# Mixture-of-experts groups that pass their slots to and fro and keep weights, with additions placed after their gathers, in a four-layer attention and expert stack

## The chip, the cores and the metric

The kernel runs on one core of one Trainium2 chip, as one launch. The metric is the device time in microseconds of that core; the time of a kernel is the median of several runs. All arithmetic is float32.

## The reference, cut to what matters

The input is an image batch of 2 x 256 channels x 32 x 32, so 2 images (b = 0, 1) of 1024 tokens with 256 features. Two convolutional attention layers come first (layers 0 and 1), and nothing in them is changed. Then the tokens `t` go through two more layers:

```python
t = t + _L2_attn_ref(_ln_t(t), ...)   # window attention
t = t + _L2_ffn_ref(_ln_t(t), ...)    # 8 experts, top 2, hidden 1024, per-expert norm
t = t + _L3_attn_ref(_ln_t(t), ...)   # additive attention
t = t + _L3_ffn_ref(_ln_t(t), ...)    # 8 experts, top 2, hidden 512
# additive attention: for each pair of tokens i, j of one image
h = jnp.tanh(q[:, :, None, :] + k[:, None, :, :] + bh)   # 1024 x 1024 x 32
e = jnp.einsum('biju,u->bij', h, Wa[:, 0]) + ba[0]
v = softmax(e) @ inputs
# experts: h = gelu(x @ W1[e] + b1[e]); y = h @ W2[e] + b2[e]; sum of the two, weighted by the gate
```

## The kernel before

The changed part is the class `Late`, which computes everything behind the window attention. It is cut into steps that are Python generators; each `yield` ends a piece. The method `run` holds a table `plan` of the steps with a start, an end and a number of pieces, and `merge` issues the pieces of all steps in order of these planned times. The unit is about a microsecond, but only the order that results counts. The names of the steps are used throughout: the first digit is the layer, the second the group of tokens. In layer 2 there are two groups, one for each image (8 tiles of 128 tokens each). In layer 3 group 0 is image 0 (8 tiles), and groups 1 and 2 are the halves of image 1 (4 tiles each).

- **D** (`dispatch`): layer norm (`norm`, `inverse_root`), a transpose by TensorE (`ps_tr`), gate logits (`ps_router`), and `route`, some sixty small VectorE instructions with one counting product on TensorE (`ps_counts`) that give each token two slots. Then each tile's rows are scattered into `slots_in` in device memory, by two indirect DMAs a tile on GpSimd's queue. Last the experts' second bias is added to the tokens (`ps_wT`, `ps_b`).
- **E** (`experts`): loops over slot tiles of 128 rows ("slots" below), 23 in a group of 8 token tiles and 15 in a group of 4; 99 in all. A slot is loaded (`xr`), transposed (`ps_x`, then `xe` on VectorE), multiplied up (`ps_h`, bias `hb` on VectorE, Gelu `h` on ScalarE), multiplied down (`ps_y`, copied to `y` on VectorE) and stored to `slots_out`. The weights of a slot's expert come by indirect DMA into one of three lanes (`ew`): lane m % 3 walks its own third of the slots in ascending order of expert, and where the expert of a lane stays the same the index is put out of bounds and nothing is loaded. Each call of `experts` takes six new weight tiles, and its first three slots always load.
- **C** (`collect`): per token tile two indirect gathers from `slots_out` (`got`, L1425, GpSimd's queue) and two scaled additions into `t` (L1438, VectorE). In layer 2 it goes on to the norm, transposes and projections (`ps_p`, `kT`, `qb`) that the additive attention of that image needs; in layer 3 `finish` transposes four tiles of `t` at a time (`ps_f`), copies them (`y_f`, one buffer) and stores 128 channels of 512 tokens by one or two DMAs.
- **A** (`additive`): one step per image. `tanh(s)` issues four ScalarE activations of 128 x 1024 (a "set"), 64 sets an image; `products(s)` the eight TensorE matmuls that reduce them (`ps_e`). The tanh tiles have 8 buffers, so ScalarE can be two sets ahead of TensorE. After sets 32, 56 and 64 the softmax of 4, 3 and 1 token tiles is taken on ScalarE (`sc_a`); for each tile follow the transposes `ps_pt`, the values `ps_v` and an addition into `t`.

TensorE and ScalarE execute in the order that `merge` wrote from A0's start on. VectorE's, GpSimd's and the DMA queues' orders, and all orders ahead of A0, are left to the framework's scheduler, which orders by its own estimates. Every engine executes its queue in order, so a waiting instruction holds all that is behind it.

```python
"C20": (self.collect(2, 0), ("E20",), 172, 205, 20),
"E21": (self.experts(2, 1), ("D21",), 172, 450, 72),
"A1": (self.additive(1), ("C21", "A0"), 506, 815, 67),
"E30": (self.experts(3, 0), ("D30",), 550, 690, 50),
"E31": (self.experts(3, 1), ("D31", "E30"), 744, 830, 34),
"E32": (self.experts(3, 2), ("D32", "E31"), 846, 905, 34),
```

Of the kernel before, what the change touches and what calls it, by code (L numbers as in the profile page):

```python
# [44 lines left out]
}  # L45
SLOT_TILES = {IT: 2 * N // TILE + E - 1, IT // 2: N // TILE + E - 1}
NTILES = SLOT_TILES[IT]

# [7 lines left out]
def slot_tile(m, n):  # L56
    return m % LANES * -(-n // LANES) + m // LANES
# [946 lines left out]
class Late:  # L1004
# [3 lines left out]
    def __init__(self, ctx, stack, t):  # L1008
# [23 lines left out]
        for n in SLOT_TILES.values():  # L1032
            run = -(-n // LANES)
            self.tiles[n] = tl(f"tiles{n}", [P, run * LANES])
            iota(self.tiles[n], [[1, run], [run, LANES]], 0, 0)
# [52 lines left out]
    def norm(self, dst, src, tiles):  # L1088
# [6 lines left out]
        yield  # L1095
# [5 lines left out]
        yield  # L1101
# [11 lines left out]
    def normed(self, key, tokens, half):  # L1113

        if half == 0:
            self.u[key] = self.early.tile([P, IT, C], F32, name="u", bufs=3)[:, : len(tokens), :]
        tiles = range(4 * half, 4 * half + 4)
        yield from self.norm(
            lambda i: self.u[key][:, i, :], lambda i: self.t[:, tokens[i], :], tiles
        )  # L1120
        self.channels(key, tiles)
        yield
# [3 lines left out]
    def gate(self, l, b, half):  # L1126
# [14 lines left out]
        yield  # L1141

    def dispatch(self, *key, done=0):
# [11 lines left out]
        nc, t = self.nc, self.t  # L1155

        before = []
        for i in range(n):
# [9 lines left out]
            yield  # L1168

        for first in range(0, n, 4):  # L1170
# [15 lines left out]
    def route(self, key, count):  # L1186
# [14 lines left out]
        yield  # L1201
        yield
        nc.scalar.activation(lg, lg, AF.Exp)
        yield
# [4 lines left out]
        for hot in (h0, h1):  # L1209
# [8 lines left out]
            yield  # L1218
# [10 lines left out]
        yield  # L1229
# [12 lines left out]
        yield  # L1242
# [17 lines left out]
        yield  # L1260
        shape_t = [P, slot_tiles, E]
        whose, index = tl("rt_whose", shape_t), tl("rt_index", [P, slot_tiles])
        nc.vector.tensor_tensor(whose, over_tokens(ends, shape_t), broadcast(self.tiles[slot_tiles][:, :slot_tiles], shape_t), ALU.is_le)
# [7 lines left out]
        same, later = tl("rt_same", [P, slot_tiles - LANES]), slice(LANES, slot_tiles)  # L1271
        nc.vector.tensor_tensor(same, index[:, later], index[:, : slot_tiles - LANES], ALU.is_equal)
        nc.vector.tensor_scalar(index, index, float(P), self.part, ALU.mult, ALU.add)
        nc.vector.scalar_tensor_tensor(index[:, later], same, float(E * P), index[:, later], ALU.mult, ALU.add)
        rows = tl("rt_rows", [P, slot_tiles], U32, 2)
        nc.vector.tensor_copy(rows, index)
        yield
# [19 lines left out]
        yield  # L1297

    def experts(self, *key):
# [11 lines left out]
        raw, turned, hidden, waiting = {}, {}, {}, []  # L1311
        loaded = [
            [sb.tile([P, WIDEST[k]], F32, name=f"ew{k}", bufs=LANES) for k in range(2)] for _ in range(LANES)
        ]

        def fetch(m, k):
            if m >= slot_tiles:
                return
            w, width = loaded[m % LANES][k], packed[k].shape[1]
# [6 lines left out]
        def inputs(m):  # L1326
            if m >= slot_tiles:
                return
            raw[m] = sb.tile([P, C], F32, name="xr", bufs=3)
            at = slot_tile(m, slot_tiles) * TILE  # L1330
            nc.sync.dma_start(out=raw[m], in_=xs[at : at + TILE, :])
# [23 lines left out]
        def up(m, k):  # L1355
            w, x = loaded[m % LANES][0], turned[m]
# [16 lines left out]
        def down(m):  # L1373
            h = hidden.pop(m)
            w2 = loaded[m % LANES][1][:, : HB * C].rearrange("p (j d) -> p j d", j=HB)
# [7 lines left out]
            at = slot_tile(m, slot_tiles) * TILE  # L1383
# [7 lines left out]
        yield  # L1391
        turn(0)
        turn(1)
        yield
        for k in range(HB // 4):
            up(0, k)
            yield
# [15 lines left out]
    def collect(self, *key):  # L1413

        nc, t, (l, b) = self.nc, self.t, key
        tokens = GROUPS[key]
        n = len(tokens)
        shares, slots = self.routes[key][1:3]
        got = {}

        def gather(i):
            got[i] = []
            for slot in slots:
                y = self.sb.tile([P, C], F32, name="got", bufs=8)
# [4 lines left out]
                got[i].append(y)  # L1429

        for i in range(4):
            gather(i)
            yield
        for half in range(n // 4):
            for i in range(4 * half, 4 * half + 4):
                to = t[:, tokens[i], :]
                for y, share in zip(got.pop(i), shares):
                    nc.vector.scalar_tensor_tensor(to, y, share[:, i : i + 1], to, ALU.mult, ALU.add)  # L1438
                if i + 4 < n:
                    gather(i + 4)  # L1440
                yield
            if l == 2:
                yield from self.normed(("a", b), tokens, half)
                self.project(b, half)
            else:
                self.finish(tokens[4 * half])
            yield

    def finish(self, first):

        nc, t, b, at = self.nc, self.t, first // IT, first % IT * P
        for c in range(CC):
            ps = self.misc([P, CH], "ps_f")
            for k in range(CH // P):
                nc.tensor.transpose(  # L1455
                    ps[:, k * P : (k + 1) * P], t[:, first + k, c * P : (c + 1) * P], self.ident
                )
            y = self.sb.tile([P, CH], F32, name="y_f", bufs=1)
            nc.vector.tensor_copy(y, ps)  # L1459
            to = self.stack.out[b, c * P : (c + 1) * P, :]  # L1460
            n = min(CH, N - SHIFT - at)
            nc.sync.dma_start(out=to[:, at + SHIFT : at + SHIFT + n], in_=y[:, :n])  # L1462
            if n < CH:
                nc.sync.dma_start(out=to[:, : CH - n], in_=y[:, n:])
# [28 lines left out]
    def additive(self, b):  # L1493
# [69 lines left out]
        for s in range(IT * G + 1):  # L1563
# [10 lines left out]
            if jobs:  # L1574
                jobs.pop(0)()
        softmax(ready)
# [6 lines left out]
    def run(self, route):  # L1583
# [4 lines left out]
        self.p_x, self.p_h, self.p_y, self.p_e = psum("lt_x", 1), psum("lt_h", 2), psum("lt_y", 1), psum("lt_e", 1)  # L1588

        plan = {  # L1590
            "D20": (route, (), -12, 0, 14),
# [116 lines left out]
```

## Time and profile before

| | us |
|---|---|
| median of 6 runs (2997.58 to 3003.34) | 3000.36 |
| the profiled execution, its own time | 2997.72 |
| its span | 2996.0 |
| TensorE matmul busy in the span | 2743.4 (92%) |
| ScalarE busy | 1926.8 (64%) |
| VectorE busy | 1967.9 (66%) |

The profiled execution lies 1.7 us above its span and 2.6 us below the median. The stages behind the window attention, by their place in the span: E20 runs from 1912 to 2094, the first tanh starts at 2140.8, the last tanh ends at 2845.5, E32's first transpose is at 2910.0, its last product ends at 2973.3. In the trace each float32 product appears as two matmul records (32 records of `ps_h` and 16 of `ps_y` for a slot of layer 2, half of each in layer 3); transposes appear once. The columns of a table of stretches are: bounds in the span, length, then busy time and count of instructions of PE (TensorE), PEld (its weight loads), DVE (VectorE), ACT (ScalarE) and POOL (GpSimd), the mean granted clock of TensorE as a share of full speed, the DMA engines' share and GB/s.

### The profile page before, as it was taken

Reading aid. Unit: us, or ns where it says so; the run is one execution under the profiler, and the core shown is the slowest. Engines: PE = TensorE matmul, PEld = TensorE weight load, DVE = VectorE, ACT = ScalarE, POOL = GpSimd, SP = SyncE. Lnnn points to the kernel's source line nnn. Section 1 sums busy time; section 2 is a strip of 40 time slices with the busy share of each in tenths; the row PEclk is TensorE's granted clock in tenths of the full one; section 3 lists DMA queues with packets and bytes.
Section 4 is the critical chain, followed back from the end, with each engine's and each line's share of the span. In section 5 each row is a group of like instructions: output and inputs, shape, how many; then the busy total and the mean of one; then the engine's idle time right before and its main releaser. Section 6 shows DMA issues by size and latency. Waiting matters only on the chain. (4 is left out here: it accounts for less than half of the span.)

```text
span 2996.0 us, 78725 instructions
## 1 busy us (share of the span) xinstructions
PE 2743.4 (92%) x33062; PEld 1744.9 (58%) x33062; DVE 1967.9 (66%) x3673; ACT 1926.8 (64%) x2835; POOL 479.1 (16%) x569
## 2 busy tenths in 40 slices
PE   7899999999999999979999877799899989996967
PEld 4466656566656666645555445698566643663656
DVE  5898989898989898748778767643422334223343
ACT  1787888887878787735555522111499788987811
POOL 3000000000000000001111123442311122323233
PEclk9999999999999999989999988799899999998978
DMA  3000000000000000011101010344321112322335
GB/s 128 2 3 3 3 3 3 3 3 3 3 3 3 3 3 3 3 54 31 23 20 23 2 27 1 133 159 152 99 78 63 41 34 70 92 73 101 99 114 149
DMA packets 185043, 135.70 MB, mean 45 GB/s; under 512 B 134176, under 2 KB 162480, under 8 KB 180336
## 3 DMA queue, kind: packets, MB, share of 16 engines
q0 software_dynamic: 36864, 85.93, 8.8%
q1 hardware_dynamic: 146384, 44.27, 6.6%
q8 instruction: 260, 4.26, 0.5%
q10 hardware_dynamic: 1440, 0.47, 0.1%
q14 instruction: 95, 0.78, 0.1%
HBM read 181.24 MB, written 29.49 MB: 70 GB/s over the span
## 5 line engine op out<-in xcount | busy, mean ns | idle before, releaser
L177 ACT ACTIVATE sc<-sc,sa_shift 128x1024 f32<-128x1024 f32 x512 | 585.2, 1148 | 50.5 <-DMA sa_shift<-sa_min 50.3
L1506 ACT ACTIVATE th<-kT,qb 128x1024 f32<-128x1024 f32 x512 | 541.2, 1135 | 90.1 <-PE ps_e L1515 77.1
L140 PE MATMUL ps_s<-kT,qT 64*32 64x512 f32 x8192 | 503.9, 595 | 9.3 <-ACT sc L150 8.5
L216 PE MATMUL ps_o<-wt,v 128*64 128x128 f32 x6144 | 502.2, 276 | 0.0
L190 DVE STREAM_TRANSPOSE wt<-sc 128x768 f32<-128x768 f32 x512 | 465.7, 943 | 0.9 <-ACT sc L177 0.9
L216 PEld LDWEIGHTS ps_o<-wt,v 128*64 128x64 f32 x6144 | 441.1, 137 | 42.5 <-issue 42.5
L150 ACT COPY sc<-ps_s 128x1024 f32<-128x1024 f32 x256 | 257.5, 1006 | 117.5 <-PE ps_s L140 42.4
L1364 PEld LDWEIGHTS ps_h<-xe,ew 128*128 128x128 f32 x2320 | 278.8, 195 | 62.2 <-issue 37.1
L161 DVE TENSOR_REDUCE sa_least<-sc 128x1 f32<-128x1024 f32 x256 | 306.0, 1195 | 1.7 <-ACT sc L150 1.7
L147 DVE TENSOR_SCALAR_CACHE_REDUCE sc<-ps_s 128x1024 f32<-128x1024 f32 x256 | 301.3, 1177 | 5.9 <-PE ps_s L140 5.9
L1364 PE MATMUL ps_h<-xe,ew 128*128 128x128 f32 x2320 | 293.6, 281 | 10.1 <-DVE xe L1343 8.6
L1515 PE MATMUL ps_e<-th,pick 128*32 128x512 f32 x2048 | 278.9, 620 | 11.1 <-DVE ir_half L1079 9.8
L1378 PE MATMUL ps_y<-ew,h 128*128 128x256 f32 x1160 | 271.5, 383 | 4.6 <-ACT h L1353 2.6
L1369 DVE TENSOR_TENSOR hb<-ps_h,ew 128x512 f32<-128x512 f32 x145 | 100.2, 691 | 240.1 <-PE ps_h L1364 199.9
L216 PE MATMUL ps_o<-wl,v_odd 128*64 128x128 f32 x2048 | 250.9, 276 | 0.0
L1378 PEld LDWEIGHTS ps_y<-ew,h 128*128 128x128 f32 x1160 | 212.4, 190 | 60.9 <-issue 18.2
L1353 ACT ACTIVATE h<-hb 128x512 f32<-128x512 f32 x145 | 90.1, 623 | 240.7 <-DVE hb L1369 240.6
L140 PEld LDWEIGHTS ps_s<-kT,qT 64*32 64x32 f32 x8192 | 126.2, 106 | 201.5 <-issue 167.9
L198 PEld LDWEIGHTS ps_t<-ident,sc 128*128 128x128 f32 x1024 | 107.4, 140 | 215.6 <-issue 166.9
L644 ACT ACTIVATE sc<-sc,l_least 128x1024 f32<-128x1024 f32 x128 | 146.7, 1147 | 126.8 <-DVE sc L631 126.4
L216 PEld LDWEIGHTS ps_o<-wl,v_odd 128*64 128x64 f32 x2048 | 220.2, 137 | 0.0
L227 POOL TENSOR_TENSOR diag<-ident,sa_rec 32x128 f32<-32x128 f32 x64 | 24.9, 389 | 1170.4 <-DVE sa_rec L224 1170.4
(277 smaller groups left out, 3499.0 us busy)
## 6 DMA issues: line engine op xcount, KB each, us to landing
xr<-slots_in SPq DMA_DIRECT2D x99, 128.0 KB, 2.4
slots_out<-y SPq DMA_DIRECT2D x99, 128.0 KB, 1.7
sa_got<-sa_least SPq DMA_DIRECT2D x512, 0.5 KB, 1.8
sa_shift<-sa_min SPq DMA_DIRECT2D x512, 0.2 KB, 1.7
slots_in<-zero POOLq DMA_DIRECT2D x46, 128.0 KB, 2.2
sa_sums<-sa_total SPq DMA_DIRECT2D x256, 1.0 KB, 1.8
kh<-kh SPq DMA_DIRECT2D x32, 128.0 KB, 2.3
qh<-qh SPq DMA_DIRECT2D x32, 128.0 KB, 2.3
```

The source lines that it names most:

```text
L140: nc.tensor.matmul(ps[r][S * c : S * (c + 1), a, :].rearrange("p (b i) -> p b i", i=S), lhsT=qT[half, p, S * i : S * (i + 1)], rhs=keys[ha ...
L147: nc.vector.tensor_scalar(scores[m][0], flat[0], 1.0, None, ALU.mult, ALU.min, accum_out=least[m // 2][:, 0, h : h + 1])
L150: nc.scalar.copy(scores[m][1], flat[1])
L161: nc.vector.tensor_reduce(least[m // 2][:, 1, h : h + 1], scores[m][1], AX.X, ALU.min)
L177: nc.scalar.activation(scores[m][r], scores[m][r], AF.Exp, bias=shift[m // 2][:, r : r + 1], scale=-1.0, accum_out=total[i][:, 2 * p + r, ...
L190: nc.vector.transpose(weights[i, h][:, 2 * p + r, :], scores[m][r][:, :DIRECT])
L216: nc.tensor.matmul(sums[i][64 * k : 64 * (k + 1)], lhsT=values, rhs=w, start=(h == 0 and j == 0 and t == 0), stop=(h == 1 and j == 1 and t ...
L644: nc.scalar.activation(scores[n][r], scores[n][r], AF.Exp, bias=least[n][:, r : r + 1], scale=-1.0, accum_out=total[n // 4][:, at : at + 1],)
L1364: nc.tensor.matmul(ps[:, j, :], lhsT=a[:, c, at : at + P], rhs=x[:, c, :], start=(c == 0), stop=(c == CC - 1),)
L1378: nc.tensor.matmul(ps, lhsT=h[:, j, :], rhs=w2[:, j, :], start=(j == 0), stop=(j == HB - 1))
L1506: nc.scalar.activation(h, keys, AF.Tanh, bias=self.qb[b][:, s // G, g : g + 1])
L1515: nc.tensor.matmul(pe[i][c * U : (c + 1) * U, a, :], lhsT=self.pick[:, k, :], rhs=h[:, a, :], start=(k == 0), stop=(k == G - 1),)
```

## The change

- **To and fro.** Groups (2, 1) and (3, 1) (`BACK`) walk their slots in descending order, with the lanes mirrored. The six weight tiles are made once in `run` and kept over all groups. `route` remembers the last expert of each lane (`latest`), and a group in `FOLLOWS` compares its first slot of each lane with it, so that these loads too are skipped where the expert is the same. This costs a memset or a comparison and three one-column copies on VectorE for each group, and two more index tables at the start.
- **Additions once gathered.** `collect` issues its gathers first, in C20 all 16 and in C32 all 8 into tanh buffers, and its additions a set number of units later, 2.5 apart; statistics, scaling, transposes and projections have places of their own. VectorE's order too is now the written one, and from E21's start instead of A0's.
- **The plan.** Each step has a start and a distance between pieces, and a `yield` may give its own. E21 runs at 2.43 up to 205 and then at 4.8 (before: 3.86). A1 needs only "A0 tanh". D30's scatter pieces are 0.5 apart, and the bias additions become steps of their own (`shift`: B30, B31, B32). E30 starts at 582 with 4.4 between its two pieces a slot (before: 550 and 2.8). E31 also needs "A1 tanh": none of it is issued before A1's last set.
- **Output tile by tile.** `finish` handles one token tile: two transposes, one copy of 128 x 256 into a buffer of `got`, one DMA (two at an image's end), of 128 columns a row instead of 512.

```diff
-def slot_tile(m, n):
-    return m % LANES * -(-n // LANES) + m // LANES
+def slot_tile(m, n, back):
+    at = m % LANES * -(-n // LANES) + m // LANES
+    return n - 1 - at if back else at
+
+def lane(m, back):
+    return LANES - 1 - m % LANES if back else m % LANES
...
+        if key in FOLLOWS:
+            nc.vector.tensor_tensor(same[:, :LANES], index[:, :LANES], latest, ALU.is_equal)
+        else:
+            nc.vector.memset(same[:, :LANES], 0.0)
+        at = {lane(m, key not in BACK): m for m in range(slot_tiles - LANES, slot_tiles)}
+        for m in range(LANES):
+            nc.vector.tensor_copy(latest[:, m : m + 1], index[:, at[m] : at[m] + 1])
...
         def fetch(m, k):
-            w, width = loaded[m % LANES][k], packed[k].shape[1]
+            w, width = self.loaded[lane(m, back)][k], packed[k].shape[1]
...
+        if l == 3:
+            for i in range(4):
+                gather(i)
+            yield 9.0 if wide else 16.0
+            for i in range(n):
+                add(i)
+                if i + 4 < n:
+                    gather(i + 4)
+                yield 2.5
+                if i == 3 and n > 4:
+                    yield 9.0
+            return
+        if wide:
+            for i in range(n):
+                gather(i)
+            yield 8.5
+            for i in range(n):
+                add(i)
+                yield 2.5
+                if i == 3:
+                    scale(0)
+                if i == 5:
+                    channels(0)
+                if i == 6:
+                    self.project(b, 0)
...
+    def finish(self, i):
+        nc, b, at = self.nc, i // IT, i % IT * P
+        ps, y = self.misc([P, CC, P], "ps_f"), self.sb.tile([P, C], F32, name="got", bufs=8)
         for c in range(CC):
...
+            nc.tensor.transpose(ps[:, c, :], self.t[:, i, c * P : (c + 1) * P], self.ident)
+        y = y.rearrange("p (c n) -> p c n", c=CC)
+        nc.vector.tensor_copy(y, ps)
+        to = self.stack.out[b].rearrange("(c p) n -> p c n", p=P)
+        n = min(P, N - SHIFT - at)
+        nc.sync.dma_start(out=to[:, :, at + SHIFT : at + SHIFT + n], in_=y[:, :, :n])
+        if n < P:
+            nc.sync.dma_start(out=to[:, :, : P - n], in_=y[:, :, n:])
...
+        self.issued.add(f"A{b} tanh")
+        yield 9.0
         softmax(ready)
...
+            "E21": (self.experts(2, 1), ("D21", "E20"), 172, lambda now: 2.43 if now < 205 else 4.8),
+            "C20": (self.collect(2, 0), ("E20",), 172, 2.0),
+            "A0": (self.additive(0), ("C20",), 211, 4.75),
+            "N30": (self.gate(3, 0, 0), ("A0 half",), 420, 6.0),
+            "C21": (self.collect(2, 1), ("E21",), 471, 2.0),
+            "A1": (self.additive(1), ("C21", "A0 tanh"), 515, 4.6),
+            "D30": (self.dispatch(3, 0, done=1), ("A0", "N30"), 515, 2.0),
+            "E30": (self.experts(3, 0), ("D30",), 582, 4.4),
+            "B30": (self.shift(3, 0), ("D30",), 650, 6.0),
+            "D31": (self.dispatch(3, 1), ("A1 half", "D30"), 725, 2.0),
+            "C30": (self.collect(3, 0), ("E30", "B30"), 790, 2.0),
+            "E31": (self.experts(3, 1), ("D31", "E30", "A1 tanh"), 825, 1.9),
+            "B31": (self.shift(3, 1), ("D31",), 780, 3.0),
+            "D32": (self.dispatch(3, 2), ("A1", "D31", "C30"), 830, 2.0),
+            "E32": (self.experts(3, 2), ("D32", "E31"), 880, 1.9),
...
-        merge(plan["A0"][2])
+        merge(plan["E21"][2])
         engines = mybir.EngineType
-        with self.tc.manual_schedule(engines={engines.PE, engines.Activation}):
+        with self.tc.manual_schedule(engines={engines.PE, engines.Activation, engines.DVE}):
```

## The prediction, made before the change was run

> **What bounds the kernel now.** First the busy time of each stage behind the window attention (stretches of the span; the columns are in the section on the profile).
>
> ```profile
> 1912.00:2094.00 182.00, 181.22 (x1227) 168.58 (x1228) 84.47 (x245) 33.00 (x50) 62.86 (x63) 0.98 0.46 157
> 2094.00:2140.80 46.80, 33.15 (x166) 25.38 (x165) 28.36 (x89) 3.18 (x6) 21.31 (x22) 0.82 0.38 125
> 2140.80:2845.50 704.70, 658.73 (x4397) 395.23 (x4395) 224.40 (x607) 606.66 (x628) 158.97 (x162) 0.96 0.23 73
> 2845.50:2910.00 64.50, 40.40 (x246) 32.20 (x244) 29.24 (x114) 8.94 (x12) 25.34 (x26) 0.80 0.26 79
> 2910.00:2973.30 63.30, 59.85 (x398) 55.13 (x398) 22.58 (x46) 10.62 (x16) 26.13 (x27) 0.96 0.66 206
> 2973.30:2996.00 22.70, 2.78 (x9) 1.47 (x8) 5.68 (x11) 0.00 (x0) 7.67 (x8) 0.56 0.25 75
> ```
>
> E20 is pure TensorE (181 of 182 us). The tanh stage has two near limits: TensorE busy 659, ScalarE 607 of 705 us. Around it lie stretches where neither works. Second, what TensorE and VectorE waited for from 1912 and 2094 on, and what ScalarE waited for in the tanh stage (total, times, longest).
>
> ```profile
> PE ps_x L1339 <- DMA xr<-slots_in: 25.7, 4, 19.5
> PE ps_tr L1110 <- DVE u L1098: 18.0, 4, 11.0
> PE ps_f L1455 <- DVE t L1438: 13.8, 4, 7.6
> PE ps_e L1515 <- DVE ir_half L1079: 9.8, 1, 9.8
> PE ps_h L1364 <- DVE xe L1343: 8.6, 1, 8.6
> PE ps_b L1181 <- DVE wT L1175: 7.5, 2, 6.7
> ...
> DVE t L1438 <- DMA got<-slots_out,rt_slot: 45.2, 43, 5.4
> ...
> ACT th L1506 <- PE ps_e L1515: 77.1, 34, 9.1
> ```
>
> VectorE stood 45.2 us at additions whose gathers had not landed; `xe`, `u` and `wT` behind them kept TensorE (18.0 + 9.8 + 8.6 + 7.5), and ScalarE ran out of tanh tiles (77.1). No row has TensorE waiting for weights. Third, the timeline at the end.
>
> ```profile
> 2971.36 1.97 PE L1378 MATMUL ps_y<-ew,h 128*128 128x256 f32 x8 [0.56 <-issue]
> 2976.33 0.97 POOL L1425 DMA_INDIRECT got<-slots_out,rt_slot  x1 [11.51 <-issue]
> 2987.97 0.48 DVE L1438 SCALAR_TENSOR_TENSOR t<-got,rt_share,t 128x256 f32<-128x256 f32 x1 [0.79 <-DMA got<-slots_out,rt_slot]
> 2989.02 0.69 DVE L1459 COPY y_f<-ps_f 128x512 f32<-128x512 f32 x1 [0.57 <-PE ps_f L1455]
> 2992.08 0.69 DVE L1459 COPY y_f<-ps_f 128x512 f32<-128x512 f32 x1 [2.37 <-DMA out<-y_f]
> ```
>
> Behind the last product come a store, eight gathers at 1.27 us, additions, and two copies through one buffer.
>
> **Prices on TensorE.** From the timeline at full clock: a slot of layer 3 is 1.78 (`ps_h`, 16 records) + 0.22 + 1.73 (`ps_y`, 8) = 3.73 us, one of layer 2 twice the products, 7.3; a group of `ps_e` 1.92; one token tile's `ps_pt` and `ps_v` 1.09 + 3.62 = 4.7. On ScalarE: a set of tanh 4.23 (541.2 us / 128), a Gelu 0.55 in a row of tanh, a table load 1.28. The counts below are those of the two programs' instruction orders.
>
> **Up to 2094: +1 us.** Layers 0 and 1 and E20's order stay. A group's `route` gains a memset or comparison and three copies, at 0.17 us (the `rt_ends` copies) 0.7 us; only D20's lie ahead of E20's first load, the others beside TensorE work.
>
> **E20's end to the first tanh: 46.8 to 48 us.** Before, 16 of E21's products `ps_y` ran here and TensorE stood 13.3 us (8.58 + 0.73 + 3.96). Now 40 do. Until the first `ps_e` group TensorE has 192 records of `ps_h` (21.4), 80 of `ps_y` (17.3), 12 `ps_x` (1.3), 16 transposes (2.3) and the projections (7.7): 50; the first tanh is 5 earlier, as half a slot stands in between; and I allow 3 because additions every 2.5 units keep step with gather pairs (2 x 1.27), so that a late first one stays late. The stage is no shorter, but takes 22 us of TensorE work out of the next.
>
> **The tanh stage: 704.7 to 652 us.** ScalarE was busy 606.7 and idle 98.0. Between the first and last tanh there are now 15 Gelus fewer (58 against 73: three slots of E21 went ahead, nine Gelus of E31 behind) and one table load fewer: 8.3 + 1.3, so 597. TensorE gives up 62 us of slots here and falls to under 600. What idle time stays:
> - the softmax stretches, where TensorE has 4 x 4.7 us extra in eight sets. Eight sets of A0 with their slots cost TensorE 50.3 and ScalarE 44.2, the next eight 38.4 against 36.0, A1's 47.5 against 43.1: 6.1 + 2.4 + 4.4 = 13;
> - A0 to A1: the norm's second half, transposes, projections and `qb` follow A0's last group: 2 (that group) + 1.3 (the maximum, ahead in VectorE's order) + 1.4 (`uT`) + 3.9 (`ps_p`) + 1.4 (`qb`) = 10;
> - E30's start, which the new plan makes worse. Before, `ps_counts` at 2509.96 was followed by E30's first transpose at 2540.74, 30.8 us for slot numbers, 16 scatters and a load, covered by seven `ps_e` groups and the bias additions. Now four groups, 17 to 18 us of tanh, stand between, the biases are gone to B30, and VectorE's maximum of A1's tile 0 stands inside `route` and waits for one of these groups (+5). TensorE stands some 17 us at `ps_x` with the groups behind it; ScalarE is two sets (8.5) ahead and loses 17 + 5 - 8.5 = 14;
> - coupling. A0's first 32 sets took 161.1 us, and summing the dearer engine over each eight sets gives 149; the new mix is less dense, so I take 6 there and 7 for the rest: 13;
> - small waits, 5.
>
> Together 55, so 652. The cover for everything moved here is tanh; where it fails, the price is one to one.
>
> **Last tanh to last product: 127.8 to 143 us.** 30 slots now (before 19): 111.9; the last `ps_e` group 1.9; tile 7's `ps_pt` and `ps_v` 4.7; D32's transposes, router and count 3.4; biases 2.6; output transposes 3.7; 128 in all. E32 took 63.3 for 15 x 3.73 = 56, so 9 go on top for 30 slots. The 24 us hole ahead of E32 (3.83 + 0.77 + 19.54) shrinks because D32 runs inside E31: from its `ps_counts` TensorE still has five down and three up products, 14.6 us, plus 2 for a late `hb`; VectorE needs 7 to the slot numbers, GpSimd eight scatters and one weight load in its queue (11.5), then landing and load 4.5: 23. So 6 remain. On GpSimd's queue C31's gathers wait for E31's stores with E32's fetches behind them; three fetches are ahead, and a fetch lands in 3.2 us of a 3.73 slot.
>
> **Tail: 22.7 to 19.3 us.** The gathers keep their pace. After the last addition come two transposes, a copy (0.42) and two DMAs for one tile; the second `y_f` copy and its wait (2.37 + 0.69 + 0.3) go: 3.4. Rows of 512 bytes, and in the last tile of 384 and 128, take the place of 2 KB rows: the 128-byte rows landed in 1.9 us, the 1920-byte rows in 2.1, so nothing is added; between ends of 0 and +2 (twice the rows in one DMA) I take 0. The Trainium skill ("DMA: Bandwidth & Descriptors", Specifications) asks for at least 512 B a transfer, and would have the last tile's rows pay a read-modify-write; by it the tail would lose a microsecond or two of its gain, and the measured landings do not show it.
>
> **Kept weights: 0.** Up to nine slots' loads fall away, but no TensorE wait on weights is there to remove.
>
> **The clock.** TensorE's granted clock is 0.80 to 0.82 in the rows with holes, 0.96 and more elsewhere; the 16 records at 2113.74 took 4.00 us instead of 1.78 after an 8.58 us hole. Filled holes return that too, and my prices at full clock contain it.
>
> **The sum.** 2094 + 1 + 48 + 652 + 143 + 19.3 = 2957, 39 below the span of 2996.0. The profiled execution's own time would be 2959, and with the 2.6 us to the median 2961.
>
> **Rivals.**
> 1. More is filled than I allow: E30's start is covered after all and the coupling disappears (-27), and E32 finds its input (-6): 2928. For it: A1's stretch 2549.7 to 2658.7 had ScalarE busy 101.5 of 109 with a denser mix. Against it: the four groups are in the order.
> 2. Slower: ScalarE's idle time does not fall. VectorE's order is now fixed, and a copy, maximum or addition that stands ahead of its operand holds every `hb` and `xe` behind it, as the 45.2 us did; E30's start then costs 50 us rather than 14, say. Since 41 us of slots went behind the tanh, the break-even is an idle time of 55 + 39 = 94 us, nearly the old 98; at 110 the time is 3016. For it: the maximum inside D30's `route`. Against it: the additions of C20 to C32 stand 8.5 to 16 units behind their gathers, and eight gathers take 10.2 us.
> 3. It does not do what it says: the lanes' experts differ at the group borders and all loads stay. Then E31 and E32 start with 3.2 us for a load on an empty lane: 2964 to 2967, no change of sign. I count it within the forecast.
>
> **How the numbers follow.** Forecast (tanh stage within 15 us of 652, tail as said: 2942 to 2985) 0.69, rival 1 0.15, rival 2 0.16, of which half ends within 0.2% or better. 0.2% (6 us) is about what a measurement of this kernel can tell from no change. So faster 0.87, same 0.04, slower 0.09. The range takes in most of rival 1 and rival 2 up to an idle time of 86: 2930 to 2992.
>
> **What would show it.** Right: ScalarE's idle time in the tanh stage between 40 and 75 us, the longest wait of TensorE in it at E30's first `ps_x`; VectorE's wait on gathers under 15 us; a wait for `xr` at E32 of 3 to 10 us; one copy behind the last addition. Wrong: ScalarE still waiting 77 us for `ps_e`, or a tanh stage over 690 us.

## The result, and the profile after

The changed kernel took 3009.42 us (median of 21 runs) against 3000.26 us for the kernel before (42 runs): a ratio of 1.0027, 95% interval 1.0022 to 1.0033. It is slower by 0.27%, where 2961 us and a gain of 1.3% were forecast. The profiled execution after has a span of 3007.8 us.

First the stages of the changed kernel, cut as in the prediction: E20, E20's end to the first tanh, the tanh stage, last tanh to last product, tail (stretch and its length; busy time and instructions of TensorE, its weight loads, VectorE, ScalarE, GpSimd; granted clock, DMA share, GB/s).

```profile
1916.00:2097.60 181.60, 181.11 (x1227) 168.53 (x1228) 84.42 (x249) 33.00 (x50) 62.56 (x62) 0.99 0.39 132
2097.60:2152.40 54.80, 46.49 (x284) 40.26 (x283) 37.38 (x102) 6.93 (x12) 25.64 (x26) 0.91 0.23 66
2152.40:2809.00 656.60, 602.43 (x4037) 346.75 (x4039) 202.61 (x561) 594.77 (x612) 137.33 (x139) 0.97 0.20 64
2809.00:2987.10 178.10, 142.67 (x891) 124.97 (x880) 74.71 (x211) 26.77 (x38) 70.09 (x71) 0.92 0.46 143
2987.10:3007.80 20.70, 2.72 (x9) 1.15 (x8) 5.73 (x13) 0.00 (x0) 7.66 (x8) 0.56 0.30 83
```

The tanh stage did shrink, from 704.7 to 656.6 us, with ScalarE idle 62 us of it. But the stretch behind it grew by 50 us, from 127.8 to 178.1. The eleven slots that were moved there are 41 us of TensorE work; TensorE is busy 143 us of the stretch and stands idle for 35. What the engines waited for, from 1912 on (total, times, longest):

```profile
ACT th L1595 <- PE ps_e L1604: 32.8, 21, 3.5
PE ps_f L1546 <- DVE t L1474: 30.0, 13, 7.7
...
PE ps_x L1372 <- DMA xr<-slots_in: 22.6, 3, 17.5
PE ps_h L1397 <- DMA ew<-in_l_up,rt_rows: 14.3, 3, 7.5
...
DVE t L1474 <- DMA th<-slots_out,rt_slot: 7.6, 5, 5.3
```

ScalarE's wait for tanh tiles fell from 77.1 to 32.8, VectorE's for gathers from 45.2 to 7.6. In their place stand two waits that the kernel before had less of or not at all: TensorE at the output transposes `ps_f` for the additions (13 times; four of them, 13.4 us, are the tail; before, 13.8 us in four times) and at `ps_h` for weights. The timeline of TensorE and VectorE shows one of the first kind, in E32.

```profile
2938.26 0.69 DVE L1402 TENSOR_TENSOR hb<-ps_h,ew 128x512 f32<-128x512 f32 x1 [1.42 <-PE ps_h L1397]
2938.87 0.41 DVE L1380 COPY xe<-ps_x 128x256 f32<-128x256 f32 x1
2939.20 1.00 DVE L1474 SCALAR_TENSOR_TENSOR t<-got,rt_share,t 128x256 f32<-128x256 f32 x2
2940.25 0.44 PE L1546 MATMUL ps_f<-ident,t 128*128 128x128 f32 x2 [1.87 <-DVE t L1474]
2940.62 1.13 PE L1207 MATMUL ps_b<-sb_l_b,wT 8*128 8x256 f32 x4
2941.67 3.61 PE L1411 MATMUL ps_y<-ew,h 128*128 128x256 f32 x8
```

The additions wait for no gather here. But in VectorE's written order the additions stand behind `hb` and `xe` of the slot, which wait for TensorE; in TensorE's the transposes stand right behind that slot's last product. So TensorE waits for hb, xe and two additions, 1.87 us, and the eight records of `ps_y` behind it take 3.61 us where 1.89 is usual.

### The profile page after: what moved, and what is told of

Read it like the earlier page. It is cut to its first block, busy times and chain, and to the rows that moved or that the text cites. A ratio compares the mean times of both kernels' runs of the same rounds, so it can differ in the third digit from the quotient of the medians.

```text
span 3007.8 us, 78776 instructions
## 1 busy us (share of the span) xinstructions
PE 2746.9 (91%) x33062; PEld 1752.3 (58%) x33062; DVE 1976.4 (66%) x3701; ACT 1926.0 (64%) x2835; POOL 480.8 (16%) x571
## 3 DMA queue, kind: packets, MB, share of 16 engines
q0 software_dynamic: 36864, 77.53, 8.0%
## 5 line engine op out<-in xcount | busy, mean ns | idle before, releaser
L1595 ACT ACTIVATE th<-kT,qb 128x1024 f32<-128x1024 f32 x512 | 540.1, 1134 | 47.2 <-PE ps_e L1604 32.8
L1397 PEld LDWEIGHTS ps_h<-xe,ew 128*128 128x128 f32 x2320 | 285.0, 198 | 69.4 <-issue 50.7
L1397 PE MATMUL ps_h<-xe,ew 128*128 128x128 f32 x2320 | 299.9, 285 | 17.6 <-DMA ew<-in_l_up,rt_rows 14.3
L1604 PE MATMUL ps_e<-th,pick 128*32 128x512 f32 x2048 | 271.4, 607 | 2.9 <-DVE rt_ends L1271 1.5
```

The costliest lines, as they stand in the source:

```text
L1397: nc.tensor.matmul(ps[:, j, :], lhsT=a[:, c, at : at + P], rhs=x[:, c, :], start=(c == 0), stop=(c == CC - 1),)
L1595: nc.scalar.activation(h, keys, AF.Tanh, bias=self.qb[b][:, s // G, g : g + 1])
L1604: nc.tensor.matmul(pe[i][c * U : (c + 1) * U, a, :], lhsT=self.pick[:, k, :], rhs=h[:, a, :], start=(k == 0), stop=(k == G - 1),)
```

## The experiments

Each kernel was timed in five rounds beside the kernel before. The kernels ran in five sets of different speed: the kernel before took 3001 and 3002 us beside the first eight kernels (the first sets) and 3026 to 3028 us beside the others (the later sets). The record numbers the chips 4, 4, 1, 4 and 11, so one number stands for sets of either speed, and what makes the later ones slower is not shown. So ratios to before are given, and a ratio is compared with the changed kernel's in sets of like speed: 1.0027 for the first, 1.0013 for the later (its own run in one of them, below). The main theory: the tanh stage's gain is real, and new waits in the written orders spend it. Rival A: the loss is the 41 us of slots that ran out of the tanh's cover, and the waits are only where it shows.

**Output transposes a piece later.** In `collect`, layer 3:

```diff
         def add(i):
...
             if l == 3:
-                return self.finish(tokens[i])
+                return
...
                 add(i)
+                yield 2.0
+                self.finish(tokens[i])
                 if i + 4 < n:
                     gather(i + 4)
-                yield 2.5
+                yield 0.5
```

> Edit: in C30, C31 and C32 the two output transposes `ps_f` of a tile are written one piece of the experts (some 2 units) behind its two additions, instead of directly behind them; nothing else. Main theory (the 48 us that the tanh stage gained are spent on new waits that the written order makes behind the last tanh): the nine `ps_f` waits on `t` of 1.4 to 2.4 us at E31's start and in E32 (16.6 us) fall under 5, the records after them run at full clock, the stretch from the last tanh to the last product goes from 178 to about 160 us, the time from 3009 to 2989 to 2995. Rival A (the loss is the 41 us of slots that now run where nothing else does; the waits are only where it shows): TensorE waits the same microseconds at `ps_h` for `xe` or at `ps_y` for `h`, and the time stays within 3 us of 3009.

Measured 2989.27 us, ratio 0.9959 (0.9945 to 0.9973). Only one stage moved: last tanh to last product 160.6 us instead of 178.1. The `ps_f` waits fell to 15.9 us, of which 13.4 are the tail; 2.9 us came back at `ps_h` for `xe`. GpSimd's queue, which the scheduler orders, has the same order as in the changed kernel, so the gain does not come from there. This is the main theory; by rival A nothing should have been won.

**C20's gathers in two parts.** The 16 gathers of C20 as `gather(0..3); yield 5.0; gather(4..7); yield 3.5`. In the changed kernel the timeline of GpSimd and TensorE at E21's fourth slot reads:

```profile
2119.99 0.95 POOL L1466 DMA_INDIRECT th<-slots_out,rt_slot  x1 [0.30 <-issue]
2121.25 1.01 POOL L1353 DMA_INDIRECT ew<-in_l_up,rt_rows  x1 [0.30 <-issue]
2122.57 1.01 POOL L1353 DMA_INDIRECT ew<-in_l_down,rt_rows  x1 [0.31 <-issue]
2123.51 1.83 PE L1397 MATMUL ps_h<-xe,ew 128*128 128x128 f32 x7 [7.55 <-DMA ew<-in_l_up,rt_rows]
```

The fetch is issued behind the sixteenth gather, and TensorE stood 7.55 us for it.

> Edit: C20's sixteen gathers are written as four tiles, 5 units of other work, and the other four tiles, so that E21's next fetches come into GpSimd's queue between them; nothing else. Main theory: the 7.55 us that TensorE stood at `ps_h` for a weight load at 2123 goes, the first tanh comes 5 to 8 us earlier and the time falls by as much, to 3001 to 3004. Rival B (additions of C20 set the first tanh, the wait for the weights only lies beside them): the later gathers hold the additions, `u` and `kT` by as much, and the time stays within 2 us of 3009.

Measured 3002.29 us, ratio 1.0006 (0.9997 to 1.0014). E20's end to the first tanh took 46.4 us instead of 54.8, TensorE's 7.55 us are gone, and the rest stayed. Main theory.

**E31 spread.** `"E31": ..., 825, 2.5` instead of `1.9`.

> Edit: E31's pieces are planned 2.5 units apart instead of 1.9, so that D32's scatters stand five slots of E31 ahead of E32's first transpose instead of two and a half; nothing else. Main theory: the waits at E32's start (2.2 + 2.2 + 6.6 + 1.1 and smaller ones, about 14 us between 2888 and 2935) fall to 5 or less, since five slots are 18.7 us of cover against 9.3; the time falls by 7 to 10 us, to 2999 to 3002. Rival C (the weight load of 6.6 us is late because E31's last fetches and E32's first stand in one queue with the scatters and with C31's gathers, whenever that is): the waits move to E31's slots and at most 3 us are won.

Measured 2996.96 us, ratio 0.9982 (0.9973 to 0.9991). Last tanh to last product 166.6 us. Around E32's start two waits for loads, 2.7 and 2.2 us, and one of 2.7 us at E31's end remain. Main theory, the gain a little beyond it.

**E30 later.** `"E30": (self.experts(3, 0), ("D30",), 602, 4.0)` instead of `582, 4.4`.

> Edit: E30 is planned at 602 instead of 582 and its pieces 4.0 apart instead of 4.4, so that nine groups of `ps_e` and not four stand between D30's count and E30's first transpose; nothing else. Main theory: TensorE's 17.5 us at E30's first `ps_x` fall under 3, ScalarE keeps its tanh through it, the tanh stage shortens by 8 to 14 us, the time to 2995 to 3001. Rival D (in the rest of A1 TensorE has no room for the denser slots, with its 4.23 us a set): what is won at E30's start is lost behind it, and the time stays within 3 us of 3009.

Measured 2996.99 us, ratio 0.9984 (0.9975 to 0.9993). The 17.5 us at E30's first `ps_x` are gone, the tanh stage took 642.9 us. Main theory; TensorE had the room.

**VectorE's order back to the scheduler.** `manual_schedule(engines={engines.PE, engines.Activation})`, as before the change.

> Edit: the changed kernel with VectorE's order left to the scheduler again, as before the change; TensorE's and ScalarE's orders stay written. Rival 2 of the prediction (the fixed order is what costs): additions, copies and maxima are placed where their operands are ready, the `ps_f` and `xe` waits shrink and the time falls to 2985 to 3000. Main theory (the fixed order pays for itself: VectorE's 45.2 us at gathers before, 7.6 now; only the place of a few pieces is wrong): the scheduler puts additions ahead of gathers that have not landed, VectorE's wait on gathers returns to 30 us or more, ScalarE's wait for `ps_e` rises, the time is 3015 to 3035.

Measured 2982.30 us, ratio 0.9932 (0.9918 to 0.9946): the main theory's number missed, and rival 2 of the prediction has its mechanism. What TensorE, VectorE and ScalarE waited for in this kernel:

```profile
ACT th L1595 <- PE ps_e L1604: 36.6, 19, 8.9
DVE t L1474 <- DMA got<-slots_out,rt_slot: 22.8, 19, 4.8
DVE t L1474 <- DMA th<-slots_out,rt_slot: 16.0, 16, 5.3
PE ps_f L1546 <- DVE t L1474: 13.4, 4, 7.6
```

VectorE waits 38.8 us for gathers again, and the tanh stage is not longer for it: 655.1 us, against 656.6 with the written order. But `ps_f` waits only in the tail, and last tanh to last product is 157.2 us. TensorE's order is the same; VectorE takes the additions well ahead, as the timeline shows at the same place of E32:

```profile
2921.86 0.38 PE L1372 MATMUL ps_x<-ident,xr 128*128 128x128 f32 x2
2922.08 0.38 PE L1546 MATMUL ps_f<-ident,t 128*128 128x128 f32 x2
2922.12 0.69 DVE L1402 TENSOR_TENSOR hb<-ps_h,ew 128x512 f32<-128x512 f32 x1 [1.42 <-PE ps_h L1397]
2922.39 1.13 PE L1207 MATMUL ps_b<-sb_l_b,wT 8*128 8x256 f32 x4
2922.73 0.41 DVE L1380 COPY xe<-ps_x 128x256 f32<-128x256 f32 x1
```

The edit reaches a second engine: GpSimd's queue is ordered by the scheduler, and nine of E32's weight loads now stand ahead of C31's eight gathers, where six stood before the edit. So not all of the 21 us won behind the last tanh need be VectorE's.

**Weights not kept.** `FOLLOWS = set()`.

> Edit: no group follows another, so that the first three loads of each group are always made; the order to and fro stays. The prediction's term (0, or 3.2 us an empty lane at E31 and E32): the loads return to 85.9 MB from 77.5, E31's and E32's first `ps_h` wait for weights, the time is 3009 to 3015. Rival (the skipped loads also free GpSimd's queue and the transfers at E21's and E32's starts): 3018 or more. Rival from below (a skipped load still stands in the queue as an instruction, and nothing waits for it): 3007 to 3010.

Measured 3017.91 us, ratio 1.0046 (1.0032 to 1.0060), above the changed kernel's 1.0027, with intervals that just touch; the time lies above the 3009 to 3015 of the prediction's term and just under the 3018 of the first rival. The loads return (85.93 MB on the software queue, against 77.53): 6.2 MB at E21's start, 2.1 MB at E31's. Those stages did not move (55.1 and 656.4 us). The stretch behind the last tanh took 187.8 us, 10 more, and they appear in E32, where both programs load the same bytes (18.00 MB from the last tanh on): where TensorE waited 0.2 and 1.1 us for weights it waits 3.4 us once, and the granted clock behind it is 0.60 in 20 us instead of 0.91. The order of GpSimd's queue differs there too: four of C31's gathers instead of two stand together ahead of the next loads, and the next load of up weights is issued at 2928.44 instead of 2926.43. Whether that is the cause was not tried.

**E31 under the tanh again.** `"E31": (..., ("D31", "E30"), 785, lambda now: 4.4 if now < 828 else 1.9)`.

> Edit: E31 no longer waits for A1's last tanh and is planned from 785, 4.4 units apart until 828 and 1.9 after; it still follows E30, so that five of its products `ps_h` and three of its `ps_y` (14 us) come ahead of the last tanh. Rival A (the loss is the slots that ran out of the tanh's cover): all of the 14 us and the waits of E31's start come back, the time is 2985 to 2995. Main theory (in the last 50 us of tanh TensorE was busy 41, so that some 8 us of room are left there; behind it the `ps_f` waits stay with other slots): the tanh stage grows by 6 to 10 us, the stretch behind it shrinks by 14 to 18, the time is 2998 to 3004.

Measured 3011.91 us, ratio 1.0031 (1.0020 to 1.0043). Both numbers missed: TensorE's busy time under the tanh rose by 10.6 us, to 613.0, and nothing was won. The tanh stage took 662.9 us, the stretch behind it 175.1. TensorE's timeline shows why it is not less:

```profile
2913.00 0.66 PE L1372 MATMUL ps_x<-ident,xr 128*128 128x128 f32 x2 [23.55 <-DMA xr<-slots_in]
```

That is E32's first transpose. D32 starts when A1 is done, and E31's slots are what covers its route and scatters. Moved ahead, they leave the old hole: before the change it was 19.5 us. Since the edit opens a hole of its own, this run speaks against rival A only in part; what speaks against it more is the run with the later transposes, and the next one, which both win time with all these slots behind the tanh.

**Four together** (transposes later, gathers in two parts, E31 spread, E30 later; VectorE's order written).

> Edit: the four edits together (output transposes a piece later, C20's gathers in two parts, E31 spread behind the tanh, E30 later). Each alone took 20.2, 7.1, 12.5 and 12.4 us off 3009.4. If each has its own stage, they add to 52 us: 2955 to 2960, which is also the time that the prediction's sum gave. Rival (E31 spread and the later transposes fill the same holes in E32, and E30 pushed back collides with E31): 2968 or more.

Measured 2963.20 us beside 3002.43, ratio 0.9867 (0.9851 to 0.9882): 1.3% under the kernel before. That is between the two expectations. The single ratios fall short of 1.0027 by 0.0177 in all, together it is 0.0160: the later transposes and E31's spread share 6.5 us of the stretch behind the last tanh (22.5 won there, 17.5 and 11.5 singly). Tanh stage and the stretch behind it in this kernel:

```profile
2143.60:2785.90 642.30, 606.57 (x4027) 345.27 (x4026) 201.60 (x560) 594.29 (x611) 136.75 (x138) 0.98 0.21 65
2785.90:2941.50 155.60, 137.75 (x896) 120.05 (x894) 74.38 (x212) 26.78 (x39) 70.61 (x71) 0.97 0.54 165
```

So the total of the prediction, 2961 us, was reachable with the change's parts in other places. That it fits so closely is partly luck: the tanh stage is 10 us under its forecast of 652, the stretch behind it 13 us over its 143.

**Free order and three edits** (without the later transposes).

> Edit: VectorE's order left to the scheduler, and with it three of the four edits (C20's gathers in two parts, E31 spread, E30 later); the output transposes stay directly behind their additions. Theory after the first runs (VectorE's written order costs some 25 us, nearly all behind the last tanh, and brings nothing in the tanh stage; the `ps_f` waits are a part of that): the 2982 of the free order alone, less 7 and 12 for the gathers and E30 and 5 to 11 for E31: 2952 to 2958. Rival (a free order fills the same holes as the three edits, so that they bring half): 2965 or more.

Measured 2995.55 us beside 3028.11, ratio 0.9892 (0.9876 to 0.9908). Set against the changed kernel's 1.0013, from another of the later sets, 0.0121 are won, less than the theory's sum; the set differs, so how the edits share the gain with the free order is not settled by this run.

**The lanes put right.** In the changed kernel, the line that notes the last experts

```diff
-        at = {lane(m, key not in BACK): m for m in range(slot_tiles - LANES, slot_tiles)}
+        at = {lane(m, True): m for m in range(slot_tiles - LANES, slot_tiles)}
```

notes, for a group that runs back, the expert of another lane than the one the next group asks for. So E32 kept nothing.

> Edit: the changed kernel, but the three last experts of a group are written down by the lane in which the next group looks for them, for groups that run back too (one line of `route`; before the edit E32 compares with the tiles of other lanes). The traces with and without kept weights differ by 6.2 MB at E21's start and 2.1 MB at E31's and by nothing at E32's, so the third group keeps none. With the edit lane 0, whose last tile in E31 and first in E32 are both the first expert's, keeps its weights: at least 1.05 MB less. Theory (E32's first load waits 6.6 us because six loads, 3.1 MB, share the transfers at 385 GB/s): the first slot starts at once, the second waits for its load, 4 to 10 us are won with the clock that the hole cost: 2999 to 3005. Rival (the input `xr` and the scatters set E32's start, the load lies beside them): within 2 us of 3009.

Measured ratio 1.0027 (1.0017 to 1.0036). The software queue moved 76.48 MB, 1.05 less, so one slot's weights are kept; no time was won, as the rival has it. (The changed kernel was not run in this set; against its 1.0013 of another later set, this would be 0.0014 slower, within the two intervals.)

> Edit: VectorE's order free, the three edits, and the lanes of the run before. If E31's spread already covers E32's loads, the kept weights add nothing: the same as the run without them, within 2 us. If the loads still bind: 4 to 8 us under it.

Measured ratio 0.9890 (0.9875 to 0.9905), against 0.9892 without it in the same set: nothing.

**One part alone on the kernel before: output tile by tile.**

> Edit: the kernel before, with one part of the change alone: each output tile is transposed, copied and stored behind its own two additions (two DMAs of 512-byte rows at most) and not four at a time. The prediction's term: 3.4 us off the tail, nothing else, 2996 to 2998 beside 3000.4. Rival E (on TensorE, whose order is written, the two transposes now stand behind one tile's additions instead of four, so that it stands at `t` in C30 and C31 as it does in the changed kernel): 3003 or more.

Measured 3022.81 us beside 3028.11, ratio 0.9982 (0.9973 to 0.9991), 5.3 us, with the forecast 3.4 inside the interval. The tail took 19.9 us against the 22.7 of the kernel before in its own set. Rival E falls: TensorE's order holds the two transposes behind one tile's additions here too, but VectorE's is free.

**E32 without its loads.**

```diff
+        if key == (3, 2):
+            nc.vector.memset(same, 1.0)
```

This kernel leaves out all weight loads of E32.

> Edit: the changed kernel, but every weight load of E32 is marked as the same and so skipped (E32 then computes with the weights that happen to lie in its lanes; it leaves out 18 of the loads' transfers or fewer). Theory (E32's start is bound by transfers: six loads of 0.52 MB issued within 6.6 us land together at 385 GB/s): the waits for `ew` in E32, 6.6 + 1.1 + 0.2 us and the half-speed records behind them, go; 8 to 14 us are won. Rival (the lane fix changed nothing since the input, the scatters and the copies set E32's pace): within 3 us of the changed kernel.

Measured ratio 1.0003 (0.9994 to 1.0012), 0.001 or 3 us under the changed kernel in that set. The software queue moved 68.08 MB, 9.45 less. In the changed kernel's first trace, six loads of E32 are under way at once, and for 5 us the DMA engines were busy throughout. The columns are those of the stages above:

```profile
2905.00:2910.00 5.00, 0.00 (x0) 0.00 (x0) 0.00 (x0) 0.00 (x0) 1.00 (x1) 0.50 0.99 385
```

Still the loads are not what E32's start waits for in the later set: without them TensorE stands 8.6 us at E31's last slot (for `y`; with them 7.8) and 4.1 us in E32 (for `hb`; with them 7.8). The theory of the transfers falls there; in the first sets this was not run.

**Free order and all four edits; four edits and the lanes; the changed kernel again.**

> Edit: the four edits together, and VectorE's order left to the scheduler. If a written order of VectorE costs something by itself, this is under the four edits with the written order (ratio 0.9867 to before) by 5 us or more: 0.985 or less. If the cost was only where a few pieces stood, which the four edits mended, the scheduler brings nothing more: 0.9867 to 0.9895 (as in the run with three edits and a free order, 0.9892, on a chip that was slower throughout).

> Edit: the four edits together with VectorE's order written, and the three last experts written down by the right lane, so that E32 keeps lane 0's weights. Candidate for the fastest version. The lane fix alone and under the free order moved nothing (1.0027 as before it; 0.9890 against 0.9892): 0.986 to 0.988. If E31's spread leaves the loads as the last bound of E32's start: 0.984 or less.

> The changed kernel itself, on the same chip as the other three, since the chips differ (the kernel before took 3001, 3002 and 3028 us in the three sets of runs). The ratio to before should be 1.0027 again, whatever the chip. If it depends on the chip by more than 0.002, gains under that are told as open.

Measured ratios 0.9891 (0.9877 to 0.9905), 0.9936 (0.9923 to 0.9949) and 1.0013 (1.0004 to 1.0022), side by side in one set. So with all four edits the free order is 0.0045, 14 us, faster than the written one (whose corrected lanes moved nothing in the one pair of runs within a set), 12 us of it behind the last tanh (152.6 against 164.6). GpSimd's queue has eleven of the loads ahead of C31's gathers in both. By the number I had written down (0.985 or less if the written order itself costs something) it would cost nothing; by its neighbour in the same set it does. And the four edits with the written order won 0.016 in the first sets and 0.0077 here. The trace of the changed kernel in the later set has waits that the first has not:

```profile
DVE hb L1402 <- remote: 21.6, 3, 8.2
PE ps_h L1397 <- issue: 16.9, 10, 7.8
DVE y L1415 <- remote: 16.7, 4, 8.2
```

"Remote" is a release that the profile can't place; these traces hold no landing times of DMAs, so that late transfers are likely but not shown. The free order's trace has such waits too (15.1 us at `hb`, 12.3 at `y`); that a written VectorE order suffers more from each, since everything behind it stands in line, is argued and not shown.

**C31's gathers in two halves**, the second freed by the first two additions; with the later transposes, and with all four.

> Edit: output transposes a piece later (as in the first run of the study, ratio 0.9959), and C31's eight gathers in two halves: four at E32's start, four some six slots later (into a buffer that the first two additions have to free). Theory (without any of E32's loads the changed kernel was 3 us faster at most, so not the transfers but GpSimd's queue sets E32's start: C31's eight gathers, 10.2 us, wait for E31's last store and stand ahead of the fetches for E32's third to fifth slots): 3 to 8 us under that run, 0.9932 to 0.995. Rival (E32's start is set by the scatters and E31's last loads, C31's gathers lie beside TensorE's slots): 0.995 to 0.997. On the slower chips, where the same programs stood up to 0.007 differently, only the trace tells: the wait for weights in E32's third to fifth slots, 6 to 8 us there, goes or stays.

> Edit: the four edits together with VectorE's order written (0.9867), and C31's gathers in two halves. Candidate for the fastest version. Theory: 2 to 6 us under the four, 0.9847 to 0.986. Rival: E31's spread already moved the scatters ahead, so that nothing waits behind the gathers: 0.986 to 0.988. On a slow chip (four edits and the lanes: 0.9936): 0.991 to 0.993 against 0.993 to 0.995.

Measured ratios 0.9954 (0.9941 to 0.9967) and 0.9950 (0.9937 to 0.9962), both in a later set. The first is in the rival's range. The wait in E32's third to fifth slots fell from 7.8 us to 3.0, as the theory had it, but the one at E31's last slot stayed at 7.4 us, and no time was won that could be told from the later transposes alone. (They were run in the first sets alone, at 0.9959.) The second is no faster than the four edits with the lanes in another later set (0.9936). What sets E32's start in the later sets stays open.

## Why the prediction was wrong

Step by step, in its own order:

- **Up to 2094, +1.** 2097.6 in the profile shown, 2095.3 to 2097.6 in the traces of the first sets. Right within that scatter.
- **E20's end to the first tanh, 48.** 54.8. The prediction counted TensorE's work and the additions' pace and not who is queued behind the sixteen gathers on GpSimd: E21's fetches, some 20 us later for it (16 at 1.27 us). With the gathers split it was 46.4, so the rest of the step held.
- **The tanh stage, 652.** 656.6, ScalarE idle 62 us against 55. The size was right, with less TensorE work in the stage (602 us, forecast under 600) and E30's start as its largest wait (17.5 us, forecast 17); the other small terms were not measured one by one. But one ground for it, VectorE's 45.2 us at gathers, was not needed: with the order free they are back at 38.8 and the stage is 655.1. So the gain comes from what that kernel still has, the slots moved out of the stage and the new orders on TensorE and ScalarE; these were not taken apart.
- **Last tanh to last product, 143.** 178.1: this is the step that failed. The work in it, 128 at full clock, was not the fault (TensorE was busy 143 at a mean granted clock of 0.92). Mis-sized was the term for what goes wrong in 30 slots with little beside them: 9 + 6 forecast, 50 measured. The 9 was small by its own ground: E32 had 7.3 us on top for 15 slots, and part of that was work counted elsewhere. And of the 6 for E32's start 2.2 came, at `xr`; but the first up weights, whose loads were counted as covered, then kept TensorE 6.6 us. Of the 35 missing, 17.5 are the output transposes behind additions (a wait that I had not looked for, though both orders were at hand), 11.5 are D32 too late in E31, with 6.5 shared, and some 12 are left: E31's start, where the last softmax waits 8.4 us for its maximum and tables are loaded at 1.28 us, is likely, and was not tried.
- **Tail, 19.3.** 20.7. The output DMAs, each of two rows per partition, landed in 1.9 to 2.8 us, median 2.3, against the 2.1 and 1.9 of the 1920-byte and the 128-byte rows before. No price for rows of 128 and 384 bytes can be told; the "microsecond or two" for a read-modify-write has no number behind it in any run.
- **Kept weights, 0.** Right at E21 and E31, where nothing moved. At E32 nothing was kept (rival 3, for one group of three), and with the lanes put right nothing was won. That the kernel without any kept weights is 0.0019 slower at E32 is not explained by its loads, as said.
- **The clock.** The range "0.80 to 0.82 in the rows with holes" leaves out the tail's row, 0.56; nothing in the sum hangs on it.

Rival 2 had the sign and the engine: VectorE's fixed order. It had the place wrong: it looked for the cost in ScalarE's idle time, whose break-even of 94 us was never near, and not where TensorE has no cover at all. The sum's remark "where the cover fails, the price is one to one" was applied to the tanh stage only; it holds most behind the last tanh, where 41 us of slots had just been put. Of the signs that were to show the forecast right, ScalarE's idle time, the wait at E30's start, VectorE's 7.6 us at gathers and the single last copy all came true; nearly all of them lay ahead of the last tanh, and so said little of the step that failed.

## What to carry to other kernels

When an engine's order becomes fixed, walk every pair of fixed orders against each other: for each instruction that waits across engines, write down what stands ahead of its releaser in the other queue, above all in stretches that one engine bounds. Work that was moved out of a covered stage may be cover for something else where it now stands; ask what it hides before it is called a loss. And a plan tuned to a few microseconds in one set of runs may hold half its gain in another (0.016 and 0.0077 here), so a scheduler's order can be worth more than a tuned one.

## What the runs showed of the hardware

- Slow products came behind waits of under 2 us, but not behind each. E32 has four such waits at `ps_f`: behind 1.87 us (at 2940) and 1.96 us (at 2959) the next eight records of `ps_y` took 3.61 and 3.51 us instead of 1.89, and the granted clock was 0.83 over the 10 us around each; behind 1.96 and 1.52 us (at 2949 and 2954) the records were at 1.99 and 1.95 us (16 of `ps_h`), and the clock was 1.00. The Trainium skill ("TensorE: Matmul & The Clock Gate", What's actually happening) puts the throttled state behind an idle window of about 3.4 us, counted by a window that runs freely; here it came twice behind single waits of about half of that, and what decides between the four is not shown.
- Six indirect loads of 0.52 MB issued within 6.6 us moved at 385 GB/s, and the up weights then landed in 6.5 us (median) instead of 2.7. The Trainium skill ("DMA: Bandwidth & Descriptors", Anatomy of one DMA) gives 2.0 us plus the bytes at 436 GB/s for one transfer, 3.2 us by estimate; that is near the 2.7 us (a median that takes in loads skipped by their index), and not near the burst's.
- The same program took 3009 us in one set and 3030 us in a later one, with the same granted clock to 0.002 and the same busy time of ScalarE in the tanh stage (594.8 and 594.9 us). Its profiled span is 18.8 us longer (3026.6 against 3007.8), 8.7 of them behind the last tanh; over the span TensorE's busy time is 9.8 us higher, VectorE's and ScalarE's within 0.5 us. Its ratio to the kernel before differed by 0.0014.
